# A four-layer graph kernel: the rank stage two blocks behind, its helpers on other engines, and the second table after the sums

## The chip, the cores and the metric

One core of one Trainium2 chip runs the whole kernel. The metric is the device time of one execution in microseconds (us); lower is better. Five engines work side by side, each through its own instructions in order: PE (TensorE matmuls; PEld are its weight loads), DVE (VectorE), ACT (ScalarE), POOL (GpSimd) and SP (SyncE, which only issues transfers here).

## What is computed

Four graph layers on 2708 nodes with 128 features and a dense 0/1 adjacency matrix A. Each layer normalises x over its features, takes the positive part, h, and adds a layer's result to x: first a graph attention, then a symmetric graph convolution, then a convolution with batch normalisation, and last a full attention. The diff touches the last one:

```
h  = max(layernorm(x), 0)
XW = h @ W
c  = XW @ a[:128];   r = XW @ a[128:]
Z1[i, j] = leaky_relu(r[i] + c[j], slope 0.01)
den = exp(Z1);   num = A @ den
att = where(num != 0, den / num, 0)
x   = x + A @ (att @ XW)
```

A @ den would be a product of 2708^3. The kernel sorts the nodes by r instead: for a given c[j] the nodes fall into those with r + c above zero and those below, and apart from the chunk of 124 nodes in which the border lies, whole chunks enter with one exponential each. So it needs the rank of each node in r, sums of A over chunks of the sorted nodes, and tables that say which rows of A to gather for each group of columns.

## The kernel before, in words

Nodes lie in T = 22 tiles of 128 (the last has 20) and NB = 6 blocks of four tiles (the last has two). Layers 0 to 2 (lines 256 to 911) stream A and its transpose in, keep the transpose as 8-bit numbers in SBUF (`adjt8`) and store it to DRAM; they end with layer 2's totals at 329 us. Nothing in them is touched. Then three stages of layer 3 follow.

**Rank stage** (lines 1123 to 1166, 329 to 398 us). The list is written by hand: everything in the `in_order()` block keeps, on each engine, the order in which the code issues it. For a block b:

- `relu_z(b)` (ACT, L963) applies layer 2's batch normalisation to a tile z of 512 columns, `turn_z(b)` (PE, L184) transposes it into PSUM bank 0, `refresh(b)` (DVE, L974 to L985) adds it to x and takes mean and variance; POOL takes the power -1/2 (L157).
- `centred(b)` (ACT, L991, four instructions) makes h, `turn_h3(b)` (PE, L180) transposes it, `project(b)` copies it out of PSUM (ACT, L1002, the tile hT) and multiplies by W and a (PE, L1008).
- `scores(b)` (DVE, L1015) leaves c and r. `factors(b)` (ACT L1046, POOL L1047) makes the scale of XW, `values3(b)` (ACT, L1054, four instructions, then a store on SP) writes XW to DRAM.
- `diag_of(b)` (POOL, L1027) puts r on a diagonal, `broadcast_r(b)` (PE, L1037, then ACT, L1040) spreads it into `row_b`, so that every partition has all r's so far. `lower_half(b)` (POOL, L1067) masks the block's own part, and `own_bits(b)` (DVE, L1079) compares it.
- `compared(t)` compares tile t's r with all earlier nodes (DVE, L1088, `bits`, three buffers). PE sums those bits over the columns' side (L1091, L1095); the sum over the rows' side is PE's for the tiles in FOLDED (L1104, L1112, read by `row_sums`, L1116) and ACT's for the others (L1107, `junk`): tiles 9, 11, 13, 15, 17, 19, 20 and 21.

In the loop (L1136 to L1165) round b projects block b and compares the tiles of block b - 1, whose `lower` was made in round b - 1; `refresh(b + 1)` stands on DVE behind `own_bits(b - 1)`. The first three blocks' z are made ahead.

**Table stage** (lines 1182 to 1486, 398 to about 466 us). This part isn't ordered by hand; a scheduler orders each engine's list. `pieces` splits a column of numbers of 32 bits into two or three of 16 (DVE, L1174 and L1178), so that products with 0/1 rows keep their precision. From the counts come `rank` (L1201 to L1209), `less` and `more` (chunk borders below or above the rank), and the weights `wts` (L1217, L1218: 22 tiles x 21 borders, six times). `sums` (PE, L1234: 132 matmuls of 450 or 452 columns) multiplies them with `adjt8`; they stand in four groups: tiles 0 to 7 early, tiles 8 to 15 after the first table, tiles 16 to 21 pair by pair of PSUM banks at the end. In between:

- the ranks' border values (`edge_v`, `edges`), how many columns fall to each chunk (`ohb`, `many`, PE L1246; `pre`, L1249 and L1251), and a chain of small DVE instructions that lays the columns out in 22 groups (L1269 to L1365), with four small matmuls (L1322, L1339) and one (L1359) in it;
- the first table: `lanes_of` makes for each tile a matrix of 128 x 128 zeros and ones (DVE, L1392, 22 instructions), `spread` the values beside it (`rhs_k`, L1398), PE multiplies them (L1410, L1414), and `row_i` (L1415) says which rows of A the POOL gathers fetch;
- the second table, the same for c (`lanes_j`, `rhs_j`, L1429, then `jt`, `c_tab`, `c_two`), stored as `ctwo_d` by SP (L1452) and read back in rows by `fetch_c` (SP, L1550);
- the chunk sums: per pair of banks a copy out of PSUM (`s_sb`, L1468, one on DVE, one on ACT), a matmul that joins the three pieces (L1469), two copies `flat` (ACT, L1475), a split in `pre_hi` and `pre_lo` (DVE, L1476, L1477), and four stores to `pre_d`, two on SP's queue and two on ACT's (L1481).

**Gather loop** (lines 1582 to 1660, 466 to 660 us). For each of the 22 groups POOL gathers rows of A (`g`, two per group, six buffers), chunk sums (`r`, from `pre_d`), and rows of XW (L1491); DVE widens g into r (L1569); ACT makes the exponentials of the first four rows from `diag` (DVE L1532, PE L1539, ACT L1510 and L1513, DVE L1522 to L1526), and PE multiplies (L1623, L1577). The last product with A follows (660 to 780 us).

Of the kernel before, what the change touches and what calls it, by code (L numbers as in the profile page):

```python
# [20 lines left out]
def binary(  # L21
# [68 lines left out]
    def acc_bank(b):  # L90
        return ps_acc.tile([P, 512], F32, tag=f"acc{b}", name=f"acc{b}")
# [854 lines left out]
    def row(name, n=NC, dtype=F32):  # L946
        return tab.tile([P, n], dtype, name=name)
# [9 lines left out]
    def relu_z(b):  # L957
        lo, hi = E0[b]
        n = len(TILES[b])
        zs3[b] = z = tabs.tile([P, 512], F32, tag="z", name="z")  # L960
        if hi - lo < n * P:
            nc.gpsimd.memset(z[:, hi - lo :], 0.0)
        nc.scalar.activation(z[:, : hi - lo], row_b[:, lo:hi], AF.Relu, bias=tot[:, 6:7], scale=tot[:, 5:6])  # L963
# [94 lines left out]

    rk = acc_bank(5)
# [63 lines left out]
    with in_order():  # L1123
        nc.vector.tensor_scalar_mul(tot[:, 2:3], tot[:, 0:1], -1.0)
        nc.vector.tensor_mul(tot[:, 5:6], vecs[:, 2:3], tot[:, 4:5])
        ts_(tot[:, 6:7], tot[:, 5:6], tot[:, 2:3], vecs[:, 3:4], ALU.mult, ALU.add)
        nc.tensor.matmul(rk[:NB, :], none_b, ones_b[:, None, :].to_broadcast([P, 4, P]), start=True, stop=False)
        nc.vector.memset(rowsum, 0.0)
        relu_z(0)
        turn_z(0)  # L1130
        relu_z(1)
        refresh(0)
        turn_z(1)
        centred(0)
        turn_h3(0)
        for b in range(NB + 1):  # L1136
            todo = list(TILES[b - 1]) if b else []
            if b < NB:
                project(b)
            if todo:  # L1140
                own_bits(b - 1)
                compared(todo.pop(0))
            if b + 2 < NB:
                relu_z(b + 2)
            if b + 1 < NB:
                refresh(b + 1)
                centred(b + 1)
            if b + 2 < NB:
                turn_z(b + 2)
            if b < NB:  # L1150
                scores(b)
                factors(b)
                diag_of(b)
                broadcast_r(b)
                lower_half(b)
            if todo:
                compared(todo.pop(0))
            if b + 1 < NB:
                turn_h3(b + 1)
            if b < NB:  # L1160
                values3(b)
            while todo:
                compared(todo.pop(0))
            if b > 1:
                row_sums(b - 2)  # L1165
        row_sums(NB - 1)
# [3 lines left out]
    def pieces(name, x, n):  # L1170
        out = []
        for i in range(n):
            h = tab.tile([P, T], BF16, name=f"{name}{i}")
            nc.vector.tensor_copy(h, x)  # L1174
            out.append(h)
            if i < n - 1:
                rest = tab.tile([P, T], F32, name=f"{name}r{i}")
                nc.vector.tensor_sub(rest, x, h)  # L1178
                x = rest
        return out  # L1180

    nc.scalar.activation(r_exp, r_of, AF.Exp)
    r_low = row("r_low", T)
    nc.scalar.activation(r_low, r_of, AF.Exp, scale=0.01)
    low_p = pieces("low_p", r_low, 3)
    exp_p = pieces("exp_p", r_exp, 3)
    node_v = tt("node_v", [P, T], node, valid, ALU.mult)
    node_p = pieces("node_p", node_v, 2)
    r_p = pieces("r_p", r_of, 3)
    c_p = pieces("c_p", c_col, 3)  # L1190
# [20 lines left out]
    less = tt("less", [P, T, NC + 1], over(rank, NC + 1), along(by_ch, NC + 1), ALU.is_lt, BF16)  # L1211
    more = tab.tile([P, T, NW], BF16, name="more")
    ts_(more, less[:, :, 1:NC], -1.0, 1.0, ALU.mult, ALU.add)
    wts = tab.tile([P, T, 6 * NW], BF16, name="wts")
    for i in range(3):
        o = 2 * NW * i
        nc.vector.tensor_mul(wts[:, :, o : o + NW], less[:, :, 1:NC], over(low_p[i], NW))  # L1217
        nc.vector.tensor_mul(wts[:, :, o + NW : o + 2 * NW], more, over(exp_p[i], NW))  # L1218
# [170 lines left out]
    def lanes_of(name, slot):  # L1389
        o = tab.tile([P, T, P], BF16, name=name)  # L1390
        for t in range(T):
            ts_(o[:, t, :], lane_b, slot[:, t : t + 1], None, ALU.is_equal)  # L1392
        return o
# [10 lines left out]
    slot_k = row("slot_k", T)  # L1404
    nc.vector.scalar_tensor_tensor(slot_k, nth, float(-CH), rank, ALU.mult, ALU.add)
    lanes_k = lanes_of("lanes_k", slot_k)
# [13 lines left out]

    ohst = tt("ohst", [P, T, NE], over(step, NE), along(lane[:, :NE], NE), ALU.is_equal, BF16)
    chunk1 = row("chunk1", T)
    nc.vector.tensor_reduce(chunk1, gej[:, :, :NC], AX.X, ALU.add)
    chunk_p = pieces("chunk_p", chunk1, 1)
    lanes_j = lanes_of("lanes_j", slot_j)
    rhs_j = spread("rhs_j", ohst, c_p + node_p + chunk_p)
    p = bank()
    for t in range(T):
        nc.tensor.matmul(p[:, : 6 * NC], lanes_j[:, t, :], rhs_j[:, t, :], start=(t == 0), stop=(t == T - 1))  # L1429
    jt = row("jt", 6 * NC)  # L1430
    nc.vector.tensor_copy(jt, p[:, : 6 * NC])
    c_tab = row("c_tab")
    nc.vector.tensor_reduce(c_tab, jt[:, : 3 * NC].rearrange("p (i b) -> p b i", b=NC), AX.X, ALU.add)
    c_chunk = jt[:, 5 * NC :]
    second = tt("second", [P, NE], chunk[:, :, 1], c_chunk, ALU.is_equal)
    gone = tt("gone", [P, NE], c_tab, second, ALU.mult)
    nc.vector.tensor_sub(c_two[:, :, 0], c_tab, gone)
    nc.vector.scalar_tensor_tensor(c_two[:, :, 0], second, -3.0e4, c_two[:, :, 0], ALU.mult, ALU.add)
    ts_(second, second, -1.0, 3.0e4, ALU.add, ALU.mult)
    nc.vector.tensor_add(c_two[:, :, 1], gone, second)  # L1440
    c_two_f = c_two.rearrange("p e h -> p (e h)")
    nc.scalar.activation(sig, c_tab, AF.Exp, scale=0.99)
    empty = row("empty")
    ts_(empty, c_chunk, 0.0, float(N), ALU.is_equal, ALU.mult)
    node_f = tt("node_f", [P, NE], jt[:, 3 * NC : 4 * NC], jt[:, 4 * NC : 5 * NC], ALU.add)
    nc.vector.tensor_add(xw_i, node_f, empty)
    FIRST = 4
    p = bank()
    nc.tensor.transpose(p[:NS, :P], c_two_f, ident)
    ctwo_t = row("ctwo_t", P)  # L1450
    nc.scalar.copy(ctwo_t[:NS], p[:NS, :P])
    nc.sync.dma_start(ctwo_d.rearrange("(s q) -> s q", q=P), ctwo_t[:NS])  # L1452
# [8 lines left out]
    for i, pair in enumerate(pairs):  # L1461
# [16 lines left out]
        for o, part_sb in ((0, pre_hi), (2 * NC, pre_lo)):  # L1478
            for h, queue in enumerate((nc.sync, nc.scalar)):
                x0 = h * HALF + lo  # L1480
                queue.dma_start(  # L1481
                    pre_d[o : o + 2 * NC, x0 : x0 + w].bitcast(F32), part_sb[64 * h : 64 * h + 2 * NC, lo:hi]
                )
    nc.scalar.activation(row_b[:, :N], row_b[:, :N], AF.Exp, scale=-0.99)
# [659 lines left out]
```

## Time and profile before

| | us |
|---|---|
| three runs: lowest, median, highest | 781.95, 782.66, 789.66 |
| the profiled execution | 782.27 |
| its span in the profile | 780.5 |
| rank stage, 329 to 398 | 69 |
| table stage, 398 to 466 | 68 |
| gather loop, 466 to 660 | 194 |

The page gives each engine's busy time, the span in forty slices, and the costliest groups of instructions. A group's line has the source line, the engine, the operation, the tile written and those read, and the count. Lines of the waits have the engine and instruction that waited, what released it, the total, the count and the longest. The chain of work that ended last is followed back from the end and is told in order of time: start, length, what. Most lines of the kernel lie in helpers (L937 is `tt`, L157 is `inv_sqrt`), so groups are read by tile as well.

### The profile page before, as it was taken

Reading aid. Unit: us, or ns where it says so; the run is one execution under the profiler, and the core shown is the slowest. Engines: PE = TensorE matmul, PEld = TensorE weight load, DVE = VectorE, ACT = ScalarE, POOL = GpSimd, SP = SyncE. Lnnn points to the kernel's source line nnn. Section 1 sums busy time; section 2 is a strip of 40 time slices with the busy share of each in tenths; the row PEclk is TensorE's granted clock in tenths of the full one; section 3 lists DMA queues with packets and bytes.
Section 4 is the critical chain, followed back from the end, with each engine's and each line's share of the span. In section 5 each row is a group of like instructions: output and inputs, shape, how many; then the busy total and the mean of one; then the engine's idle time right before and its main releaser. Section 6 shows DMA issues by size and latency. Waiting matters only on the chain.

```text
span 780.5 us, 8324 instructions
## 1 busy us (share of the span) xinstructions
PE 661.7 (85%) x2754; PEld 416.9 (53%) x2754; DVE 586.7 (75%) x1068; ACT 452.2 (58%) x658; POOL 263.2 (34%) x218
## 2 busy tenths in 40 slices
PE   5899969878899989657749948889899999999995
PEld 3433324326687767434426615556555556667784
DVE  5999779869857966536779757776877778876972
ACT  5667677558847644244560128758667667764442
POOL 3320000231102100034410547887777777600000
PEclk9999999999999999978978959989999999999997
DMA  9699999468244797000000425556665655759702
GB/s 339 246 396 424 424 426 383 184 249 305 118 179 158 258 353 249 1 14 28 27 8 1 106 82 140 157 147 153 159 165 119 146 152 158 186 161 336 276 26 63
DMA packets 49734, 146.29 MB, mean 187 GB/s; under 512 B 13602, under 2 KB 28446, under 8 KB 41254
## 3 DMA queue, kind: packets, MB, share of 16 engines
q1 hardware_dynamic: 28966, 85.11, 30.9%
q10 hardware_dynamic: 4684, 34.73, 12.5%
q0 software_dynamic: 16032, 25.83, 12.4%
q8 instruction: 24, 0.39, 0.2%
q14 instruction: 28, 0.23, 0.1%
HBM read 126.81 MB, written 18.77 MB: 187 GB/s over the span
## 4 chain that ended last, share of the span: by engine, by line
PE 25%; DVE 21%; issue 18%; DMA 16%; ACT 7%; POOL 6%; POOLq 0%; ACTq 0%; DVEq 0%
DMA g<-adjt_d,row_i 11%; PE acc L614 7%; PE acc L1739 6%; DVE chk L695 3%; DVE r L1569 3%; PE acc L1577 3%; PE bank L1623 3%; DVE m L483 2%; DMA adj_d<-a 2%; DVE e L1602 2%; DMA r<-pre_d,pre_i 2%; PE acc L1234 2%; ACT y L474 1%; POOL rstd L157 1%; ACT adjt L216 1%
## 5 line engine op out<-in xcount | busy, mean ns | idle before, releaser
L1623 PE MATMUL bank<-r,d_hi 128*128 128x512 f32 (+1 forms) x264 | 143.8, 549 | 25.1 <-DMA r<-pre_d,pre_i 14.5
L1624 ACT ACTIVATE ln<-bank,tiny 128x512 f32<-128x512 f32 x132 | 83.8, 634 | 71.9 <-PE bank L1623 33.1
L1577 PE MATMUL acc<-e,xw 128*128 128x512 f32 (+1 forms) x264 | 122.2, 551 | 0.0
L340 PE MATMUL acc<-tau,hw 128*128 128x512 f32 (+1 forms) x240 | 100.0, 563 | 12.4 <-DVE tau L348 12.3
L1491 POOL DMA_INDIRECT g<-adjt_d,row_i x44 | 86.6, 1968 | 39.1 <-DVE row_i L1415 26.0
L1623 PE MATMUL bank<-r,d_lo 128*128 128x512 f32 (+1 forms) x264 | 99.3, 380 | 0.0
L1569 DVE CAST r<-g 124x2708 fp32r<-124x2708 fp8e4 x44 | 68.0, 1573 | 41.4 <-DMA g<-adjt_d,row_i 11.3
L1623 PEld LDWEIGHTS bank<-r,d_hi 128*128 128x128 f32 x264 | 51.0, 193 | 67.4 <-issue 34.4
L481 ACT CAST m<-a 128x660 fp32r<-128x660 fp8e4 (+1 forms) x45 | 55.2, 1233 | 53.4 <-PE acc L1739 31.2
L340 PEld LDWEIGHTS acc<-tau,hw 128*128 128x128 f32 x240 | 43.6, 193 | 70.5 <-issue 44.2
L1491 POOL DMA_INDIRECT r<-pre_d,pre_i x44 | 64.8, 1474 | 47.5 <-PE bank L1623 22.4
L348 DVE SCALAR_TENSOR_TENSOR tau<-row_b,sg,a 128x1536 f32<-128x1536 f32 (+1 forms) x44 | 70.8, 1624 | 11.9 <-DMA a<-in_adj_dram 11.9
L1602 DVE SCALAR_TENSOR_TENSOR e<-row_b,sig,ln 128x1536 f32<-128x1536 f32 (+3 forms) x46 | 71.5, 1561 | 7.6 <-PE bank L1623 6.1
L157 POOL TENSOR_TENSOR rstd<-isq,neg_half 128x4 f32<-128x4 f32 (+1 forms) x24 | 29.1, 1214 | 128.3 <-DVE isq L156 83.6
L371 ACT ACTIVATE a<-a 128x2708 fp8e4<-128x2708 f32 x22 | 54.1, 2458 | 24.1 <-issue 11.3
L695 DVE SCALAR_TENSOR_TENSOR chk<-chk 128x2708 f32<-128x2708 f32 (+1 forms) x22 | 65.6, 2982 | 3.0 <-DMA chk<-in_adj_t_dram 3.0
L1623 PEld LDWEIGHTS bank<-r,d_lo 128*128 128x128 f32 x264 | 51.0, 193 | 28.7 <-issue 24.4
L1596 ACT ACTIVATE ln<-ln 128x512 f32<-128x512 f32 (+2 forms) x68 | 62.8, 926 | 0.6 <-ACT ln L1624 0.6
L1577 PEld LDWEIGHTS acc<-e,xw 128*128 128x128 f32 x264 | 48.4, 191 | 12.8 <-issue 3.8
L483 DVE CAST m<-a 128x2048 fp32r<-128x2048 fp8e4 (+1 forms) x43 | 39.5, 920 | 20.8 <-PE acc L614 10.8
L614 PE MATMUL acc<-m,y_hi 128*128 128x512 f32 (+1 forms) x132 | 49.8, 384 | 5.2 <-DVE m L600 2.0
L614 PE MATMUL acc<-m,h_hi 128*128 128x512 f32 (+1 forms) x132 | 53.8, 415 | 0.1
(438 smaller groups left out, 1259.9 us busy)
## 6 DMA issues: line engine op xcount, KB each, us to landing
a<-in_adj_dram SPq DMA_DIRECT2D x21, 1354.0 KB
adjt<-in_adj_t_dram ACTq DMA_DIRECT2D x12, 1354.0 KB
chk<-in_adj_t_dram ACTq DMA_DIRECT2D x11, 1354.0 KB
chk<-in_adj_t_dram SPq DMA_DIRECT2D x10, 1354.0 KB
a<-in_adj_t_dram SPq DMA_DIRECT2D x9, 1354.0 KB
adj_d<-a POOLq DMA_DIRECT2D x22, 338.5 KB
adjt_d<-adjt SPq DMA_DIRECT2D x5, 1354.0 KB
a<-adj_d SPq DMA_DIRECT2D x5, 1024.0 KB
```

Source lines behind the costliest of these rows:

```text
L340: nc.tensor.matmul(accs[b][:, : hi - lo], stationary, tau[b // 3][:, o : o + hi - lo], start=first, stop=last)
L348: nc.vector.scalar_tensor_tensor(tau, row_b[:, h0:h1], sg[:, t : t + 1], tiles_a[t][:, h0:h1], ALU.max, ALU.mult)
L481: nc.scalar.copy(m[:, : hi - lo], src[:, lo:hi])
L614: nc.tensor.matmul(sums_of[phase, b][:, : hi - lo], part[:, t, :], tiles_m[k][:, lo - base : hi - base], start=t == 0 and i == 0, stop=t = ...
L695: lambda: nc.vector.scalar_tensor_tensor(a[:r], a[:r], 1.0, a[:r], ALU.is_equal, ALU.not_equal, accum_out=odd[:r, t : t + 1])
L1491: return nc.gpsimd.indirect_dma_start(out=out, out_offset=None, in_=src, in_offset=bass.IndirectOffsetOnAxis(ap=idx, axis=0),)
L1569: ins = nc.vector.tensor_copy(rows_r[q][:CH], g[:CH])
L1577: m = nc.tensor.matmul(ys_acc[b][:, : hi - lo], xws[s], waiting[s][:, lo:hi], start=(s == 0), stop=(s == NE - 1))
L1596: pin(nc.scalar.activation(lns[s][:, lo:hi], lns[s][:, lo:hi], AF.Exp, scale=-1.0))
L1602: nc.vector.scalar_tensor_tensor(waiting[s][:, lo:hi], row_b[:, lo:hi], sig[:, s : s + 1], lns[s][:, lo:hi], ALU.max, ALU.mult)
L1623: pin(nc.tensor.matmul(num[:, : hi - lo], d, a[:, lo:hi], start=(i == 0), stop=(i == 3)))
L1624: pin(nc.scalar.activation(lns[s][:, lo:hi], num[:, : hi - lo], AF.Ln, bias=tiny))
```

## The change

Five edits, all between the end of layer 2 and the gather loop:

1. The rank stage's loop runs over i from -3 to NB + 1. Round i projects block i, centres block i + 1, refreshes block i + 2, makes z of block i + 3 and compares block i - 2. z has one buffer, not two. In a round the first comparison follows the projection, the second stands ahead of the broadcast, and `diag_of` stands ahead of `factors`.
2. `pieces` runs on POOL. Those of r and c are issued inside the last rounds, from i = NB on, those of the node numbers ahead of the stage.
3. `less`, `more` and `wts` are made for tiles 0 to 7 and then for tiles 8 to 21.
4. `lanes_of` makes the rows of the first n_act tiles on ACT: |lane - slot| for each tile, then max(1 - that, 0) in one instruction. All 22 of the first table, 14 of the second.
5. The block that builds the second table stands behind the pairs of sums and their stores, not ahead of them.

Its core (the moved block of the second table is left out where it is unchanged):

```diff
-        zs3[b] = z = tabs.tile([P, 512], F32, tag="z", name="z")
+        zs3[b] = z = tabs.tile([P, 512], F32, tag="z", name="z", bufs=1)
...
+    def pieces(name, x, n):
...
+            nc.gpsimd.tensor_copy(h, x)
...
+                nc.gpsimd.tensor_sub(rest, x, h)
...
+    r_low = row("r_low", T)
+    node_v = tt("node_v", [P, T], node, valid, ALU.mult)
+    node_p = pieces("node_p", node_v, 2)
...
-        relu_z(0)
-        turn_z(0)
-        relu_z(1)
-        refresh(0)
-        turn_z(1)
-        centred(0)
-        turn_h3(0)
-        for b in range(NB + 1):
-            todo = list(TILES[b - 1]) if b else []
-            if b < NB:
-                project(b)
+        for i in range(-3, NB + 2):
+            todo = list(TILES[i - 2]) if i > 1 else []
+            if 0 <= i < NB:
+                project(i)
+            if -1 <= i < NB - 1:
+                centred(i + 1)
             if todo:
-                own_bits(b - 1)
+                own_bits(i - 2)
                 compared(todo.pop(0))
-            if b + 2 < NB:
-                relu_z(b + 2)
-            if b + 1 < NB:
-                refresh(b + 1)
-                centred(b + 1)
-            if b + 2 < NB:
-                turn_z(b + 2)
-            if b < NB:
-                scores(b)
-                factors(b)
-                diag_of(b)
-                broadcast_r(b)
-                lower_half(b)
+            if i + 3 < NB:
+                relu_z(i + 3)
+            if 0 <= i < NB:
+                scores(i)
+                diag_of(i)
+                factors(i)
+            if 0 <= i + 2 < NB:
+                refresh(i + 2)
+            if i + 3 < NB:
+                turn_z(i + 3)
             if todo:
                 compared(todo.pop(0))
-            if b + 1 < NB:
-                turn_h3(b + 1)
-            if b < NB:
-                values3(b)
+            if 0 <= i < NB:
+                broadcast_r(i)
+                lower_half(i)
+            if -1 <= i < NB - 1:
+                turn_h3(i + 1)
+            if 0 <= i < NB:
+                values3(i)
+            if i == NB:
+                nc.scalar.activation(r_exp, r_of, AF.Exp)
+                nc.scalar.activation(r_low, r_of, AF.Exp, scale=0.01)
+                low_p = pieces("low_p", r_low, 3)
+                exp_p = pieces("exp_p", r_exp, 3)
+                r_p = pieces("r_p", r_of, 3)
+                c_p = pieces("c_p", c_col, 3)
             while todo:
                 compared(todo.pop(0))
-            if b > 1:
-                row_sums(b - 2)
+            if i > 2:
+                row_sums(i - 3)
...
+    for ts in (slice(0, 8), slice(8, T)):
+        n = ts.stop - ts.start
...
+        nc.vector.tensor_tensor(
+            less[:, ts], each(rank, NC + 1), by_ch[:, None, :].to_broadcast([P, n, NC + 1]), ALU.is_lt
+        )
+        ts_(more[:, ts], less[:, ts, 1:NC], -1.0, 1.0, ALU.mult, ALU.add)
+        for i in range(3):
+            o = 2 * NW * i
+            nc.vector.tensor_mul(wts[:, ts, o : o + NW], less[:, ts, 1:NC], each(low_p[i], NW))
+            nc.vector.tensor_mul(wts[:, ts, o + NW : o + 2 * NW], more[:, ts], each(exp_p[i], NW))
...
-    def lanes_of(name, slot):
+    def lanes_of(name, minus_slot, n_act, slot=None):
...
-        for t in range(T):
+        far_off = tab.tile([P, T, P], BF16, tag="far_off", name="far_off")
+        for t in range(n_act):
+            nc.scalar.activation(far_off[:, t, :], lane, AF.Abs, bias=minus_slot[:, t : t + 1])
+        nc.scalar.activation(o[:, :n_act, :], far_off[:, :n_act, :], AF.Relu, bias=ones[:, 0:1], scale=-1.0)
+        for t in range(n_act, T):
             ts_(o[:, t, :], lane_b, slot[:, t : t + 1], None, ALU.is_equal)
...
-    lanes_k = lanes_of("lanes_k", slot_k)
+    lanes_k = lanes_of("lanes_k", minus_k, T)
...
+    lanes_j = lanes_of("lanes_j", minus_j, 14, slot_j)
```

On the engines' lists this leaves, in the end: on ACT the last count (`junk` of tile 21) still stands behind the exponential of row_b (L1484), as before; on PE 30 sums stand ahead of the matmuls of `many` (11 before) and 18 between those of `pre` and L1322 (37 before); 54 follow the first table without a break, then pair 0's join, 14 sums, pair 1's, 7 sums, pair 2's, and only then the second table's products. On DVE the copy `s_sb` of pair 0 stands behind the last `rhs_j`, and `jt` between `pre_hi` and `pre_lo` of pair 2. On SP the six stores to `pre_d` stand ahead of that of `ctwo_d`.

## The prediction, made before the changed kernel ran

> **What bounds the kernel now.** I read the page for the whole, then the windows for the stages, then the waits and the chain inside the two stages that the diff touches. Times are microseconds from the start of the span; a letter in brackets is a block (0 to 5) or a tile (0 to 21).
>
> ```profile
> span 780.5 us, 8324 instructions
> PE 661.7 (85%) x2754; PEld 416.9 (53%) x2754; DVE 586.7 (75%) x1068; ACT 452.2 (58%) x658; POOL 263.2 (34%) x218
> ...
> PEclk9999999999999999978978959989999999999997
> ```
>
> ```profile
> 329.00:398.00 69.00, 50.20 (x316) 28.07 (x316) 40.38 (x123) 36.63 (x85) 25.64 (x25) 0.85 0.07 22
> 398.00:420.00 22.00, 11.34 (x77) 7.47 (x77) 17.92 (x95) 5.36 (x5) 1.23 (x1) 0.69 0.00 1
> 420.00:440.00 20.00, 20.00 (x123) 14.29 (x122) 19.15 (x78) 0.80 (x2) 8.42 (x6) 1.00 0.23 54
> 440.00:460.00 20.00, 11.90 (x58) 4.95 (x56) 8.44 (x25) 6.42 (x15) 3.76 (x3) 0.79 0.37 109
> ```
>
> The windows' columns are length, then busy PE, PEld, DVE, ACT, POOL, then clock and DMA. Rank stage (329 to 398) and table stage (398 to 466) take 137 us in which no engine is full except PE and DVE at 420 to 440. They are bound by handing over:
>
> ```profile
> DVE own L1079 <- POOL lower L1067: 19.2, 6, 5.2
> ACT row_b L1040 <- PE acc L1037: 19.2, 6, 3.9
> ...
> PE acc L1037 <- POOL diag L1027: 12.6, 6, 3.4
> ```
>
> Vector waits 19.2 of 69 us for the GpSimd half-matrix of the block just projected; what stands behind that wait is `refresh` of the next block, so all engines turn in one ring per block (the six `own` start at 343.12, 352.00, 361.17, 371.66, 382.00, 391.74: 9.7 each). The chain shows what ends each stage:
>
> ```profile
> 398.02 2.35 ACT row_b L1484
> 400.37 2.44 ACT junk L1107 x2
> 403.66 0.69 DVE less L937
> ...
> 417.30 7.17 PE acc L1234 x37
> ...
> 438.06 3.43 DVE rhs_j L1398 x6
> ...
> 455.31 2.25 DMA pre_d<-pre_lo
> ...
> 459.76 6.28 DMA r<-pre_d,pre_i
> ```
>
> The rank waits for the last count on ScalarE (to 402.8); I call the start of `less` R (403.66). Then R+20.7 (424.40) is the matmul pair L1322 behind 37 sums; R+25.9 is `row_i` (429.51); R+37.7 the end of `rhs_j` (441.40); R+51.6 the end of the last `pre_lo` (455.28); R+61.1 (464.78) the first matmul of the gather loop, R+62.5 that of its second row.
>
> **Part 1, comparisons two blocks behind.** Vector no longer meets a half-matrix made in the same round: `own` finds one that is a round old. The 19.2 us go, and the next ring limits. I follow it by the start of the copy hT (L1002), with durations of the DVE, ACT and PE rows. z has now one buffer: z(1) waits for the transposes of z(0) (331.3), z(2) stands on ACT behind four `centred` (334.65), and its transposes (to 336.6) stand on PE ahead of those of h(0): hT(0) goes from 335.30 to 337.65, a loss of 2.35. Round 0 then is hT 0.6, projection 2.1 (half clock, as in the row at 335.94), scores 0.3, the add of refresh(2) 0.7, transposes of z(3) 0.6, broadcast 1.1, copy row_b 0.55, four xw 1.1 = 7.05: hT(1) 344.7. Round 1 has the projection at 1.1 and the rest alike: 6.0, hT(2) 350.7. In round 2 the second comparison stands ahead of the broadcast and its bits behind refresh(4): 6.0 - 0.65 + 1.4 + 0.3 + 0.3 = 7.35, hT(3) 358.05. Round 3: refresh(5) 1.35, bits 0.55, comparison 0.95 in place of the add and transposes: 7.55, hT(4) 365.6. Round 4: tile 7 is still on PE (projection ends 367.5), tiles 8 and 9 2.0, broadcast behind a slowed diagonal 1.25, row_b 0.6, xw 1.15, the count of tile 11 1.4 ahead of the copy: hT(5) 373.9. Before it was 384.81. Round 5 is PE: 0.45 + 0.7 + tiles 12, 13 2.65 + broadcast 0.7 + tiles 14, 15 3.1, to 381.5; Vector has bits of 16 at 381.8, of 19 at 386.2, of 20 at 388.8, of 21 at 390.4. On ScalarE: count of 19 from 386.25 to 388.5, count of 20 388.85 to 391.2, the exponential of row_b 2.4, the last count 2.45: 396.1 in place of 402.8. The order of those last two doesn't change. So -6.6.
>
> The row against a rule: after an idle of 2.12 us on PE the row at 370.43 gives four transposes 1.06, the one at 344.62 (the same work at full clock) 0.61. The Trainium skill (TensorE: Matmul & The Clock Gate, Part 1) wants an idle window of some 3.4 us for the half clock. My rounds leave PE idle for 1.7 to 2.1 at most. By the rule nothing is lost after round 0, by the row each such gap can cost about 1.6 (3.2 us at half rate). I charge 1.0: rank stage -5.6 (by the rule -6.6, by the row at three gaps -1.8).
>
> **Part 2, the 16-bit pieces on GpSimd.** Twenty Vector instructions leave the end of the stage, about 0.085 apart, 1.7 us. Worth nothing: Vector there waited 2.74 us for the last count. They come back as twenty GpSimd instructions of 22 columns from 385.6 on (when r_exp is there), ten of them ahead of the weights at R. The Trainium skill (GPSIMD Engine Reference, the opening ahead of section 1) calls GpSimd the wrong place for elementwise work, about half of Vector's rate; that is 20 x 0.33 = 6.6 from Vector's 0.16. The trace has `factor` (4 columns) at 0.20 alone and 1.37 beside Vector's bits: 4 to 27 us in all, the first ten 2 to 14. I take 1.4 until the bits end (390.4) and 0.35 after: the ten end at 393, R is 397. Cost nothing while the ten end before R; if the cover were gone, R moves by the excess.
>
> **Part 3, weights for eight tiles first.** less 0.24 + 0.37, more 0.17, six products of 168 columns at 0.23: the first sum starts at R+2.4 and not R+4.8. The second halves cost six more starts, and `edge_v` ends at R+7.6, not R+6.7; `many` goes from R+11.2 to R+11.8. But PE now has 30 of the 48 first sums done ahead of `many` (11 before), the first ten at half clock (0.4), the others 0.2; so L1322 has 18 ahead of it, not 37: R+14.2 + 18 x 0.2 = R+17.8, and Vector's part is ready at R+16. Gain 2.9.
>
> **Part 4, unit rows on ScalarE.** lanes_k leaves Vector (22 x 0.165 = 3.6). On ScalarE 22 Abs of 128 columns at 0.3 (as L991, four in 1.28), pre_sb between, one Relu of 2816 columns 2.55: from R+8.3 to R+18.1; its matmuls come at R+20.6. Hidden by 2.5; without that cover each us would go to row_i. `row_i` R+22.9. For lanes_j eight stay on Vector (1.3), 14 Abs and a Relu of 1792 (4.2 + 1.7) end at R+32.7, beside Vector's rhs_j to R+32.2 (5.5 earlier).
>
> **Part 5, all sums, then the second table.** PE has 54 sums in a row (10.5 from R+22.7), so pair 0 is done at R+32.7, and the copies s_sb wait for Vector's rhs_j and ScalarE's Relu, both to about the same instant. Then pair 0: joint 0.9, flat 1.1, pre_hi 0.4, pre_lo 0.6 to R+36.0; pair 1's joint after 14 sums at R+37.85; the last sums at R+39.2, s_sb R+39.9, joint R+40.85, flat R+41.9, pre_hi, jt, pre_lo: R+43.25 for R+51.6. Before, the copy s_sb of pair 2 stood on ScalarE behind a DMA issue that waited for pre_lo (2.15); now only that of pre_hi(1) is ahead. The six pre_d stores on SP and six on ScalarE's queue go out ahead of ctwo_d on SP: ctwo_d is late by 3 against R, but its readers c_row (SP) wait for it only till R+47.7, needed at about R+58. What is late next is the second table: jt R+42.4, c_two R+44.7, diag there, and from diag to the second d_lo 7.05 as before (455.38 to 462.4): R+51.75, widen(0) R+53.3. The gather of r starts behind the matmul L1539 as its row says (R+47.9) and lands 6.0 later: R+53.9. First loop matmul R+54.0 for R+61.1: -7.1, say -7.0 with the instant where three engines meet.
>
> **Sum.** -5.6 - 7.0 = -12.6. From 466 on nothing changes, and the first gathers of g are issued 9 us earlier, with more lead. Against the profiled execution (782.27, of which the span is 780.5) that makes 769.7; its time is 0.4 below the median shown (782.66), so 770.1 on the median. 1% is 7.8 us, about what can be told from no change.
>
> **Rivals.** (a) 48%: the sum, 770.1 (767 to 774). (b) 18%: more. No clock loss (-6.6), the r gather waits for its stores alone (R+46.5, 1.4 sooner, with widen(0) at R+53.3 then the limit): -14.5, 768; up to 763 if lanes and sums meet better. (c) 22%: part of it is lost. Either PE falls to half clock in three rounds (-1.8 for the rank), or the gather loop gives some back: the chain from 470 to 560 is 32.7% gathers of g, single ones 5.9 to 14.6 us, so an earlier start needn't come through whole. -5 to -9: 774 to 778. Against it: the gathers are issued when the loop frees their buffers, so they move with it. (d) 6%: no change, if the stage was bound by the counts on ScalarE (14.9 us of `junk` plus 2.4) all along; against it, ScalarE is 36.6 of 69 busy. 782. (e) 6%: slower, by GpSimd: `pow` on 22 columns took 3.88 there. At 3.5 each the first ten end at 420.6, R would be 23 later than planned: 793. It decides from 2.5 each (ten from 385.6 to 410.6, which eats the 12.6); the nearest rows say 0.2 to 1.4.
>
> Range 764 to 778: (a), (b) and most of (c). Faster by over 1% (below 774.8): (a), (b) and a third of (c), 0.75; within 1%: 0.18; slower: 0.07.
>
> **What would show it.** Waits of own for lower near nothing; hT(5) at about 374; last `junk` ending at 396 to 397; a first sum 2.4 after less; L1322's successor 17.8, row_i 22.9, last pre_lo 43 and the first loop matmul 54 after less. Wrong if PE's clock in the rank stage falls below 0.85, if `wts` waits for GpSimd, if s_sb waits for ScalarE's Abs, or if the loop is longer than its 194 us (466 to 660).

## The result, and the profile after

| | before | after |
|---|---|---|
| median of 13 runs each (lowest to highest), us | 783.54 (777.24 to 789.66) | 773.99 (768.75 to 781.47) |
| ratio after to before | | 0.9882, 95% interval 0.9848 to 0.9915 |
| the profiled execution, us | 782.27 | 772.65 |
| its span | 780.5 | 770.9 |

The change saves 1.2%, about 9.3 us. The prediction had 12.6 us (770.1). A few executions of each kernel take over 1.5% longer than its fastest, and the ratios leave them out; the one profiled with edit 3 undone (784.2 us) is of these.

Line numbers from here on are those of the kernel whose trace is shown, mostly the changed one; behind line 1059 most lie 5 to 17 above the ones used so far, and those of the pairs of sums 23 below.

The head of the changed kernel's page, engine by engine, and the row of the granted clock:

```profile
span 770.9 us, 8331 instructions
...
PE 664.5 (86%) x2754; PEld 419.4 (54%) x2754; DVE 580.9 (75%) x1017; ACT 467.6 (61%) x696; POOL 276.7 (36%) x242
...
PEclk9999998989999999957979969999999999899998
```

Work has moved from VectorE (586.7 to 580.9 us busy) to ScalarE (452.2 to 467.6) and GpSimd (263.2 to 276.7). The four windows of the prediction, now of the changed kernel (length, then busy PE, PEld, DVE, ACT, POOL, then clock, DMA share, GB/s):

```profile
329.00:398.00 69.00, 51.88 (x320) 30.05 (x320) 41.07 (x115) 40.90 (x86) 32.24 (x46) 0.80 0.07 22
398.00:420.00 22.00, 18.04 (x114) 12.36 (x115) 19.76 (x99) 10.16 (x26) 1.48 (x2) 0.80 0.00 1
420.00:440.00 20.00, 19.31 (x110) 12.01 (x109) 14.20 (x43) 9.71 (x23) 11.39 (x6) 1.00 0.37 102
440.00:460.00 20.00, 8.37 (x38) 4.92 (x39) 11.72 (x25) 5.58 (x15) 10.26 (x7) 0.69 0.34 84
```

From 398 to 420 PE is busy 18.0 us and not 11.3: the sums start sooner. But in the rank stage the granted clock is 0.80, where it was 0.85. The waits of that stage (who waited for what: total, times, longest) no longer have a line of `own` for `lower`, which was the longest before. What has grown is VectorE's wait for PE's projection. The line before, then three lines of the changed kernel:

```profile
DVE rc L1015 <- PE bank L1008: 5.7, 6, 2.1
```

```profile
DVE rc L1015 <- PE bank L1008: 21.5, 11, 4.5
ACT row_b L1040 <- PE acc L1037: 15.1, 5, 4.5
POOL diag L1027 <- DVE rc L1015: 10.3, 5, 3.9
```

ScalarE's wait for the broadcast (`row_b`) isn't new, it was 19.2.

At the far end, PE's list in order of time shows how the gather loop starts (start, length, line, what; in brackets the idle time ahead of it and what ended it):

```profile
446.09 1.12 PE L1551 MATMUL bank<-diag,ones 128*128 128x512 f32 x2 [0.77 <-DVE diag L1544]
453.90 0.76 PE L1635 MATMUL bank<-r,d_hi 128*128 128x512 f32 x1 [6.69 <-DMA r<-pre_d,pre_i]
...
456.88 0.77 PE L1635 MATMUL bank<-r,d_hi 128*128 128x512 f32 x1 [1.79 <-DMA r<-pre_d,pre_i]
```

The first matmul of the loop's second row, 456.88, stood at 466.18 before:

```profile
466.18 0.77 PE L1623 MATMUL bank<-r,d_hi 128*128 128x512 f32 x1 [0.21 <-DMA r<-pre_d,pre_i]
```

It comes 9.3 us sooner. From there to the end of the span it is 314.0 us, and it was 314.3. So in this pair of traces what was won ahead of the loop came through.

Two marks make runs comparable, as single executions differ by up to 4 us before the rank stage and by several us behind the loop's start: the time from the first z (the start of `relu_z(0)` on ScalarE) to R (the start of `less` on VectorE), and that from R to the matmul of the second row.

| us | before | predicted | after |
|---|---|---|---|
| first z to R | 74.34 | 68.7 | 69.35 |
| R to first sum | 4.8 | 2.4 | 2.7 |
| R to the row behind L1327 | 21.6 | 17.8 or just after | 18.6 |
| R to row_i | 25.9 | 22.9 | 22.8 |
| R to the end of rhs_j | 37.8 | 32.2 | 31.9 |
| R to the end of the last pre_lo | 51.6 | 43.25 | 44.3 |
| R to the first r gather | 54.9 | 47.9 | 48.05 |
| R to the second row | 62.5 | 55.4 | 57.6 |

### The profile page after: what moved, and what is told of

It reads as the page before. It is cut to its first block, busy times and chain, and to the rows that moved or that the text cites. A ratio compares the mean times of both kernels' runs of the same rounds, so it can differ in the third digit from the quotient of the medians.

```text
span 770.9 us, 8331 instructions
## 1 busy us (share of the span) xinstructions
PE 664.5 (86%) x2754; PEld 419.4 (54%) x2754; DVE 580.9 (75%) x1017; ACT 467.6 (61%) x696; POOL 276.7 (36%) x242
## 5 line engine op out<-in xcount | busy, mean ns | idle before, releaser
L340 PE MATMUL acc<-tau,hw 128*128 128x512 f32 (+1 forms) x240 | 101.8, 572 | 12.7 <-DVE tau L348 12.7
L1503 POOL DMA_INDIRECT g<-adjt_d,row_i x44 | 91.8, 2086 | 23.4 <-issue 12.5
L1635 PEld LDWEIGHTS bank<-r,d_hi 128*128 128x128 f32 x264 | 51.5, 195 | 66.3 <-issue 32.2
L1503 POOL DMA_INDIRECT r<-pre_d,pre_i x44 | 59.3, 1348 | 36.9 <-PE bank L1635 14.7
L483 DVE CAST m<-a 128x2048 fp32r<-128x2048 fp8e4 (+1 forms) x43 | 39.5, 920 | 18.9 <-PE acc L614 8.8
L372 POOL DMA_DIRECT2D adj_d<-a x22 | 12.3, 558 | 115.0 <-ACT a L371 115.0
```

The costliest lines, as they stand in the source:

```text
L340: nc.tensor.matmul(accs[b][:, : hi - lo], stationary, tau[b // 3][:, o : o + hi - lo], start=first, stop=last)
L1503: return nc.gpsimd.indirect_dma_start(out=out, out_offset=None, in_=src, in_offset=bass.IndirectOffsetOnAxis(ap=idx, axis=0),)
L1635: pin(nc.tensor.matmul(num[:, : hi - lo], d, a[:, lo:hi], start=(i == 0), stop=(i == 3)))
```

## The experiments

The theory to test: the sum was right in its parts, and what is missing was lost in two places, PE's half clock in the first rounds and the landing of the second r gather. The rivals are in the expectations. Each kernel was also timed against the kernel before (783.2 to 784.0 in these groups).

### PE kept busy in the first rounds

```diff
+    def warm(n):
+        for _ in range(n):
+            nc.tensor.matmul(
+                rk[:NB, :], none_b, ones_b[:, None, :].to_broadcast([P, 4, P]), start=False, stop=False
+            )
...
+        warm(14)
         nc.vector.memset(rowsum, 0.0)
...
                 project(i)
+                if i < 3:
+                    warm(4)
...
                 turn_z(i + 3)
+                if i < -1:
+                    warm(4 * (i + 4))
...
                 turn_h3(i + 1)
+                if i < 3:
+                    warm(5)
```

> The changed kernel with TensorE kept busy through the first rounds of the rank stage by matmuls of zero weights into the bank of counts (adding nothing): 14 ahead of the first z, 4 to 12 behind each of the first transposes, 4 behind each projection and 5 behind the transposes of h, in rounds 0 to 2. Theory 1 (the rank stage fell short of the sum because TensorE ran at half clock in rounds 0 to 2, granted clock 0.50 to 0.84 from 329 to 360): the projection of round 0 takes 1.1 and not 2.1, the transposes 0.6 and not 1.08, the broadcasts 1.1 and not 1.91; the last hT comes 3 to 5 us earlier than 376.7, R (the start of less, 399.28) comes 2 to 4 us earlier, and the time is 770 to 772 where the changed kernel has 774. Theory 2 (ScalarE's order sets the rounds: copy of row_b, four xw, then hT, whatever the clock): the last hT and R move by less than 1 us and the time is 774 within 1.

Measured: 770.41, ratio 0.9799 (0.9734 to 0.9865). First z to R 64.05, 5.3 less than in the changed kernel's trace. PE's list of the changed kernel:

```profile
330.80 1.11 PE L184 MATMUL acc<-ident,z 128*128 128x128 f32 x4 [3.69 <-ACT z L963]
...
338.74 2.10 PE L1008 MATMUL bank<-w_ext,hT 128*128 128x130 f32 x8 [0.68 <-ACT hT L1002]
341.78 1.08 PE L184 MATMUL acc<-ident,z 128*128 128x128 f32 x4 [0.94 <-DVE xs L974]
342.65 1.91 PE L1037 MATMUL acc<-diag,ones 128*128 128x512 f32 x2
...
346.76 1.16 PE L1008 MATMUL bank<-w_ext,hT 128*128 128x130 f32 x8 [1.34 <-ACT hT L1002]
348.86 1.08 PE L184 MATMUL acc<-ident,z 128*128 128x128 f32 x4 [0.94 <-DVE xs L974]
```

And the same work with the zero weights in between (L1140 are the added matmuls):

```profile
338.39 1.16 PE L1008 MATMUL bank<-w_ext,hT 128*128 128x130 f32 x8
339.48 1.03 PE L1140 MATMUL acc<-ones_b,none_b 128*6 128x512 bf16 x4
340.49 0.63 PE L184 MATMUL acc<-ident,z 128*128 128x128 f32 x4
340.98 1.12 PE L1037 MATMUL acc<-diag,ones 128*128 128x512 f32 x2
```

Each instruction takes about half: 2.10 to 1.16, 1.08 to 0.63, 1.91 to 1.12. The windows from 330 to 345 and from 345 to 362 have a clock (the third number from the end) of 0.50 and 0.70 in the changed kernel, and of 1.00 here; the first two lines are the changed kernel's:

```profile
330.00:345.00 15.00, 9.52 (x33) 6.91 (x34) 6.40 (x35) 6.61 (x15) 4.24 (x5) 0.50 0.01 1
345.00:362.00 17.00, 11.93 (x49) 6.58 (x48) 7.00 (x32) 9.48 (x31) 8.96 (x10) 0.70 0.10 31
```

```profile
330.00:345.00 15.00, 12.99 (x70) 6.48 (x68) 6.76 (x38) 9.12 (x24) 5.47 (x6) 1.00 0.02 7
345.00:362.00 17.00, 14.36 (x92) 7.65 (x90) 10.29 (x46) 8.44 (x27) 9.79 (x12) 1.00 0.14 42
```

Theory 1 holds: added work makes the stage shorter, because the rounds wait for PE. VectorE's wait for the projection falls from 21.5 to 16.7 us.

The start of the hT copies, from the first z, shows the rounds:

| us from the first z | hT(0) | (1) | (2) | (3) | (4) | (5) | R |
|---|---|---|---|---|---|---|---|
| before | 6.0 | 13.3 | 22.1 | 31.7 | 44.3 | 55.5 | 74.3 |
| predicted, without the charge for the clock | 8.3 | 15.4 | 21.4 | 28.7 | 36.3 | 44.6 | 67.7 |
| after | 8.2 | 16.2 | 23.3 | 31.5 | 38.9 | 46.8 | 69.35 |
| after, PE kept busy | 6.8 | 13.2 | 19.0 | 26.2 | 33.6 | 41.4 | 64.05 |

At full clock the rounds last 6.3, 5.9, 7.2, 7.4 and 7.8 us; the sum had 7.05 (its projection at half clock), 6.0, 7.35, 7.55 and 8.3.

### The same matmuls in the old loop

The edit is the same `warm`, at the same places of the old loop of the kernel before.

> The kernel before with the same matmuls of zero weights in the first three rounds of its old loop, nothing else. From the first z to R it had 74.34. Theory 1 (edit 1's own worth is what the sum said, 5.6 to 6.6, at full clock, and the half clock takes 2.5 of it away in the changed kernel, but less in the old loop, whose ring of VectorE and GpSimd has slack for TensorE): 71.5 to 74 from the first z to R, against 64.05 of the changed loop with the same matmuls, so edit 1 is worth 7.5 to 10 at full clock; 781 to 783.5. Rival (the clock is worth the same 6 us in either loop): 67.5 to 69, and 777 to 778.

Measured: first z to R 74.13, where it was 74.34, though the clock from 330 to 345 is 1.00 now and was 0.70. VectorE still waits for GpSimd's half-matrix, 20.0 us for 19.2:

```profile
DVE own L1079 <- POOL lower L1067: 20.0, 6, 5.0
```

Theory 1 holds for the stage: the old ring of VectorE and GpSimd covered PE's half clock, the new one has no such cover. At full clock edit 1 is worth 74.13 - 64.05 = 10.1 us, more than the sum had.

The time is another matter: 777.75, ratio 0.9955 (0.9931 to 0.9979), is the rival's 777 to 778, some 3.5 us less than before, and in the trace only 0.6 of that lies ahead of the second row. What made the rest isn't settled. Behind the second row the four traces with zero weights have 308 to 311.5 us, the others 309.8 to 319.3 (318.5, that with edit 3 undone, among them). So of what the zero weights save in the time, here and in the changed kernel, only the part in the marks is accounted for.

### Edit 1 alone, and all but edit 1

The first is the kernel before with the new loop and `bufs=1` for z. The second is the changed kernel with the old loop, in whose last round the pieces are issued:

```diff
-        for i in range(-3, NB + 2):
...
+        relu_z(0)
+        turn_z(0)
+        relu_z(1)
+        refresh(0)
+        turn_z(1)
+        centred(0)
+        turn_h3(0)
+        for b in range(NB + 1):
...
+            if b == NB:
+                nc.scalar.activation(r_exp, r_of, AF.Exp)
...
+                c_p = pieces("c_p", c_col, 3)
             while todo:
```

> The kernel before with edit 1 alone (the new loop and the single z). The 16-bit pieces stay on VectorE behind the stage, the tables as before. Theory 1 (the five edits add up, edit 1 is worth what the trace of the changed kernel shows at R): R 398.7 to 399.9 for 403.66, the second row of the gather loop at 461.2 to 462.4 (466.18 before), 778.5 to 779.5 where the kernel before has 783.5. Rival (the pieces of VectorE, 1.7 us, come onto the path as VectorE is full from 380 to 395 in the new order): R at 400.5 to 401.5 and 780 to 781.

> The changed kernel with the rank stage's loop as before (comparisons one block behind; z has one buffer, as two don't fit beside edit 2's tiles), edits 2 to 5 kept. Theory 1: R at 403.5 to 404.5, from R to the second row of the gather loop 57 to 58 us as in the changed kernel (57.6; 62.5 before), 778 to 779.5. Rival (the pieces on GpSimd need the new order: in the old one they stand behind the last lower of the ring and end after the last count): the weights wait for GpSimd and R to the first sum takes over 3 us; 780 or more.

Measured: edit 1 alone 778.17, ratio 0.9936 (0.9908 to 0.9964), first z to R 71.53; all but edit 1 782.1, ratio 0.9969 (0.9937 to 1.0001), first z to R 74.77 and R to the second row 60.2.

Edit 1 alone gives 5.0 us in the time. R follows the last count by 0.87 us, as before (0.86), so VectorE's 16-bit pieces did not come onto the path, and the rival is out. In its trace the stage gained only 2.8, at a clock of 0.59 and 0.50 in the two windows. Six traces of the new loop without zero weights and with the exponential in its place have 67.83 to 71.53 from the first z to R, mean 69.9; three of the old loop (one with zero weights) have 74.13 to 74.77, mean 74.4. So edit 1 is worth 4.5 on average, and it varies by 3.7 from execution to execution; the old loop varies by 0.6. The stage follows the clock from 345 to 362: 67.83 us at 0.87, 69.01 and 69.35 at 0.70, 70.74 and 70.83 at 0.60, 71.53 at 0.50.

Without edit 1, the other four gave 2.4 us (the interval runs from 4.9 to nothing), where 4 to 5.5 were expected, and R to the second row is 60.2 and not 57 to 58. The rival of this run has its mechanism shown, at a smaller price than the 3 us that it named: GpSimd's list and VectorE's behind R (405.19).

```profile
404.49 1.23 POOL L1442 MEMSET flat<- 128x1354 f32 x1 [11.16 <-ACT junk L1122]
405.66 0.34 POOL L1063 CAST low_p<-r_low 128x22 bf16<-128x22 f32 x1
```

```profile
406.75 0.34 DVE L1227 TENSOR_TENSOR wts<-less,low_p 128x168 bf16<-128x168 bf16 x1 [0.38 <-POOL low_p L1063]
407.62 0.33 DVE L1228 TENSOR_TENSOR wts<-more,exp_p 128x168 bf16<-128x168 bf16 x1 [0.52 <-POOL exp_p L1063]
408.34 0.34 DVE L1228 TENSOR_TENSOR wts<-more,exp_p 128x168 bf16<-128x168 bf16 x1 [0.39 <-POOL exp_p L1063]
```

In this order of GpSimd's list the memset of `flat` stands ahead of the pieces, and it waits for the last count. The pieces start 0.5 behind R, the weights wait for them, and the first sum comes at R + 4.3 and not R + 2.7. This is the cover that the prediction named for edit 2 (the ten pieces end before R): in the changed kernel the tenth ends at 393.96, 5.3 ahead of R, though one of them took 1.59 us:

```profile
391.23 1.59 POOL L1063 CAST exp_p<-r_exp 128x22 bf16<-128x22 f32 x1
...
393.76 0.20 POOL L1063 CAST exp_p<-exp_pr 128x22 bf16<-128x22 f32 x1
```

### The exponential behind the last count

```diff
         row_sums(NB - 1)
+        nc.scalar.activation(row_b[:, :N], row_b[:, :N], AF.Exp, scale=-0.99)
...
-    nc.scalar.activation(row_b[:, :N], row_b[:, :N], AF.Exp, scale=-0.99)
```

> The changed kernel with the exponential of row_b (2.44 us of ScalarE, which stands ahead of the last count) behind the last count. Theory 1 (the end of the rank stage is ScalarE's chain of counts): the last count ends at 396.1 and not 398.5, R comes 2.4 us earlier, and the whole of it reaches the end: 771.6 where the changed kernel has 774. Rival (VectorE's bits or the 16-bit pieces on GpSimd end about there too): R gains less than 1 us and the time stays at 774 within 1. Rival 2 (the tables take up the gain, since ScalarE starts the unit rows later): R gains 2.4 but the first matmul of the second row of the gather loop less than 1.2.

Measured: 774.17, ratio 0.9877 (0.9826 to 0.9927), no difference from the changed kernel that these intervals can show. The end of ScalarE's list in the changed kernel, and then in this one:

```profile
393.65 2.44 ACT L1496 ACTIVATE row_b<-row_b 128x2708 f32<-128x2708 f32 x1
396.00 2.43 ACT L1122 ACTIVATE junk<-bits 20x2688 bf16<-20x2688 bf16 x1
```

```profile
396.34 2.44 ACT L1122 ACTIVATE junk<-bits 20x2688 bf16<-20x2688 bf16 x1
...
398.79 2.44 ACT L1184 ACTIVATE row_b<-row_b 128x2708 f32<-128x2708 f32 x1
```

From the copy hT(5) to R it is 20.4 where the changed kernel has 22.6: the 2.2 are there. But in this execution the rounds lasted 1.2 longer (half clock again), and the second row came at R + 58.4. From the first z to the second row only 0.25 us is left (126.70 for 126.95), less than the 1.2 of rival 2; but `row_i` stands at R + 22.8 as in the changed kernel, so its reason, later unit rows, isn't what took the gain. The place is shown, the worth in the time only together with the clock, below.

### Edits 2 to 5 undone one by one

Pieces on `nc.vector` behind the loop; `for ts in (slice(0, T),)` for the weights; `lanes_of` with `n_act` 0 and `slot_k`, `slot_j` again; the block of the second table moved ahead of `pairs`.

> The changed kernel with edit 2 undone: the 16-bit pieces on VectorE, issued behind the rank stage as before. Theory 1 (worth nothing in itself, VectorE waits for the last count on ScalarE): R comes where it did against the last count (0.76 behind it), from R to the first sum 2.7, to the second row of the gather loop 57.6, and 774 within 1.5. Rival (the twenty of VectorE, 1.7 us, come onto the path, as VectorE's bits now end later against the counts): R is 1 to 1.7 us later against the last count, 775 to 776.

> The changed kernel with edit 3 undone: less, more and the weights for all 22 tiles in one go. Theory 1: the first sum starts at R + 4.8 and not R + 2.7, many falls to R + 11.3, the row behind the matmuls L1327 comes at R + 21.5 and not R + 18.6, row_i at R + 25.7, and the second row of the gather loop at R + 60.5 and not R + 57.6; 777. Rival (with the unit rows on ScalarE, VectorE reaches many sooner and fewer first sums stand ahead of it): own_beg within 1 us of R + 18.6 and the time stays at 774 to 775.

> The changed kernel with edit 4 undone: all 44 unit rows on VectorE. Theory 1: the end of rhs_j goes from R + 31.9 to R + 34.2 to R + 37.5 (14 instructions at 0.165 for certain, the other 22 as far as VectorE had no wait there), and the second row of the loop moves as much, 2.3 to 5.6 us: 776 to 779. Rival (lanes_k lies in VectorE's wait for the matmuls L1327, and ScalarE's two Relu of 2.6 and 1.7 us set as much as they save): less than 1.5 us, 774 to 775.

> The changed kernel with edit 5 undone: the second table ahead of the pairs of sums. Theory 1 (edit 5 brings the last pre_lo forward by what the table cost the pairs, but puts the second table last): the last pre_lo comes at R + 45 to R + 46 for R + 44.3, the r gathers go out at R + 48.5 to R + 49.5 for R + 48.05, but c_two is done by R + 36, so that the row behind them is as in the kernel before, 10.9 behind the last pre_lo, at R + 56 to R + 57: edit 5 is worth nothing or costs 1 us, 773 to 774. Rival (the sum as predicted, edit 5 carries the gain of the last pre_lo): the last pre_lo at R + 48 to R + 51, the second row of the loop at R + 60 to R + 62, 777 to 779.

| undone | time, ratio (interval) | R to row behind L1327 | end of rhs_j | last pre_lo | first r gather | second row | first r gather to second row |
|---|---|---|---|---|---|---|---|
| none | 773.99, 0.9882 (0.9848 to 0.9915) | 18.6 | 31.9 | 44.3 | 48.05 | 57.6 | 9.55 |
| 2, pieces | 774.71, 0.9878 (0.9847 to 0.9909) | 18.6 | 32.2 | 44.4 | 47.8 | 58.0 | 10.1 |
| 3, weights | 776.46, 0.9900 (0.9824 to 0.9975) | 21.9 | 35.2 | 47.6 | 51.4 | 60.9 | 9.5 |
| 4, unit rows | 776.52, 0.9900 (0.9859 to 0.9941) | 18.9 | 38.7 | 44.4 | 47.6 | 58.0 | 10.5 |
| 5, table last | 775.21, 0.9894 (0.9864 to 0.9923) | 18.8 | 32.2 | 46.6 | 50.5 | 58.4 | 7.9 |

The times differ by less than their intervals; the marks decide. With edit 3 undone only the marks from R are used. They agree with the two other kernels that make the weights in one go, the kernel before and that with edit 1 alone: the first sum at R + 4.8 in all three, the row behind L1327 (L1322, L1317) at R + 21.9, 21.6 and 21.6.

Edit 2 is worth nothing, as the sum had it: R is 0.77 behind the last count and was 0.76, and the 0.4 at the second row lies in the landing of the gathers (last column). Edit 3 is worth 3.3 us (60.9 - 57.6), for 2.9 in the sum: with it undone, PE does 35 sums without a break ahead of the matmuls L1327.

```profile
417.14 6.93 PE L1239 MATMUL acc<-adjt,wts 128*126 128x452 fp8e4 x35
424.00 0.40 PE L1327 MATMUL bank<-ahead,ones 22*128 22x22 f32 x2
```

Edit 4 is worth 0.4 at the second row once edit 5 is there, and that too lies in the landing: undone, the gathers go out 0.45 sooner. So its rival holds in the marks (less than 1.5). Undone, rhs_j ends 6.8 later, but that costs nothing ahead of the last pre_lo, as VectorE's list then has the copies of the sums in between the rhs_j:

```profile
434.69 0.65 DVE L1404 TENSOR_TENSOR rhs_j<-ohst,c_p 128x484 bf16<-128x484 bf16 x1
435.26 0.62 DVE L1441 COPY s_sb<-acc 126x452 f32<-126x452 f32 x1
435.80 1.22 DVE L1404 TENSOR_TENSOR rhs_j<-ohst,c_p 128x484 bf16<-128x484 bf16 x2
```

Edit 5 brings the last pre_lo and the r gathers forward by 2.4 us, and the second row by 0.8 only; R + 58.4 lies between what theory 1 (56 to 57) and the rival (60 to 62) had. Between the two stands the landing of the gathers: 7.9 us from issue to use with the table early (7.3 to 7.6 in three traces with the old order of the tables), 9.3 to 10.5 in eight traces with the table last.

### The c_row reads behind the gathers

With the table last, SyncE issues the first read of `c_row` and GpSimd the first gather of r within 0.4 us of each other. SyncE's list, then GpSimd's, in the changed kernel:

```profile
446.99 0.35 SPq L1562 DMA_DIRECT2D c_row<-ctwo_d  x1
```

```profile
447.33 0.89 POOL L1503 DMA_INDIRECT r<-pre_d,pre_i  x1 [11.78 <-PE bank L1551]
448.53 0.88 POOL L1503 DMA_INDIRECT r<-pre_d,pre_i  x1 [0.30 <-issue]
```

The reads lead by 0.34 us here, and with edit 4 undone by -0.17. Where the landing took 7.3 to 7.9, they led by 1.0 (before, edit 1 alone) or 3.5 (table early). The edit:

```diff
-        nc.sync.dma_start(p, ctwo_d[s0 * P : (s0 + 2) * P].partition_broadcast(P))
+        src = ctwo_d[s0 * P : (s0 + 2) * P].partition_broadcast(P)
+        if pool:
+            pin(nc.gpsimd.dma_start(p, src))
+        else:
+            nc.sync.dma_start(p, src)
...
-        fetch_c(FIRST + 2 * s)
+        fetch_c(FIRST + 2 * s, True)
...
-            fetch_c(coming + 4)
+            fetch_c(coming + 4, s == 0)
```

> The changed kernel with the first three reads of c_row (128 KB each) issued by GpSimd behind the four gathers of r and two of xw, not by SyncE at the same instant as the first r (446.99 and 447.33). Theory 1 (with edit 5 the second r gather lands 2 us later against its issue because the c_row reads lie ahead of it in the DMA queues): from the first issue of an r gather to the matmul of the second row 7 to 8 us, not 9.3 to 10.5, that row at R + 55.3 to R + 56 and 772 to 773. Rival (it is the gathers themselves, or the three c_row issues hold up GpSimd's next gathers): 9.3 to 10.5 as before, or the loop behind longer by 1 us or more; 774 to 775.5.

Measured: 773.11, ratio 0.9831 (0.9773 to 0.9889); the second row at R + 55.7, 7.6 behind the first gather. PE's list:

```profile
452.12 0.77 PE L1639 MATMUL bank<-r,d_hi 128*128 128x512 f32 x1 [5.77 <-DVE r L1585]
...
453.55 0.80 PE L1639 MATMUL bank<-r,d_hi 128*128 128x512 f32 x1 [0.24 <-DVE r L1585]
```

PE now waits for VectorE's widening of g (`r`, L1585) and no longer for the gather. Theory 1 holds for the mark. In the time the 1.9 us can't be told from the changed kernel; the stretch behind the second row was 319 us in this execution and 308 in the last kernel below, which has the same edit. One price shows: ScalarE now waits for c_row, 2.6 us here and 2.0 there, and starts the exponentials from it at R + 62.0 and R + 61.8, where the changed kernel had R + 61.1. Whether that takes part of the gain back isn't shown.

### The two together

The first has `warm` and the exponential last, the second the c_row reads too.

> The changed kernel with TensorE kept busy in the first rounds and the exponential of row_b behind the last count, both edits as run singly. If they add up (each acts at its own place: hT at the beginning, the last count at the end): from the first z to R 61.6 to 62.3 (64.05 with the first alone), 767.5 to 769.5. If VectorE's bits end the stage once the rounds are short: 63 to 64 and 770.

> As warm_exp, and the c_row reads behind the r gathers too. If the c_row reads delay the second r gather: 1.5 to 2 us less than warm_exp, 766 to 768. If not, the same as warm_exp within 1 us.

Measured: 762.17, ratio 0.9743 (0.9690 to 0.9795), and 763.04, ratio 0.9755 (0.9708 to 0.9803). First z to R is 61.87 and 61.84: the two edits of the rank stage add up (64.05 less 2.2). The second row comes 8.0 behind the first gather with the c_row reads behind, 10.1 without, and again the time doesn't show it. Both are faster than the changed kernel, whose interval begins at 0.9848, by about 1.3%. That is 3 to 5 us less time than was expected of them (767.5 to 769.5, 766 to 768); the marks don't account for it, as with the zero weights in the old loop.

## Why the prediction was right, and where it fell short

The sign and the range held: faster, 774.0 in 764 to 778. The time lies at the border of the sum's band (a) and of rival (c), a part lost, and of the signs of being wrong one came: the clock of the rank stage, 0.80 where 0.85 was the limit. Of the marks, hT(5) came at 376.7 for 374 and the last count at 398.5 for 396 to 397. (By its own chances faster by over 1% is 0.73, not 0.75.) Point by point:

- Part 1. The wait of `own` for `lower` is gone, and the last count sets R: right. The step that failed is "I charge 1.0". The prediction had the row (four transposes at 1.06 for 0.61 behind an idle of 2.12) and the rule of the Trainium skill (TensorE: Matmul & The Clock Gate, Part 1: half rate after an idle window of about 3.4 us, full again after as long a busy one), and took little from either. What it left out is the way back: it let each gap cost a fixed 1.6. PE was idle 3.69 us ahead of the first transposes, then every round kept it idle for 0.6 to 1.5 us, and it ran at half clock until 346. It was full for one projection after 3.6 us of unbroken work (341.78 to 345.4), half again two idles of 1.34 and 0.94 later, full for the next projection after 3.5 us (348.86 to 352.4), and half again. The busy part of the rule agrees with this, the idle part doesn't: no idle after the first was over 2.1. Nor did the half clock come with the idle itself: the first work behind it was still at full clock (the broadcasts at 368.44 before, the projection at 346.76 after), the slow transposes 2 us later. The right charge was 69.9 - 67.7 = 2.2 on average against the sum's own rounds, and 5.8 against rounds at full clock throughout (69.9 - 64.05), mostly because the sum also had half clock ahead of hT(0) and in round 0's projection. So the clock part of rival (c), given as -1.8 for the rank, came true in part: -4.5 on average for -5.6.
- Part 2. Worth nothing, cover as named; the run without edit 1 shows the price without it, 1.6 us. The 22-column operations took 0.20 to 0.31 alone and 1.37 and 1.59 beside VectorE's bits (389.68 to 392.74), close to the estimate of 0.35 and 1.4; the 0.33 from half of Vector's rate fits only those that ran alone.
- Part 3. The largest part of the tables: 3.3 for 2.9.
- Part 4. The sum gave it lanes_k and the earlier end of rhs_j. The end of rhs_j did move by 5.9, but with the table last nothing of the loop's start hangs on it; worth 0.4 at most.
- Part 5. The last pre_lo came at R + 44.3 (43.25), the gathers at R + 48.05 (47.9). The step that failed is "lands 6.0 later": the first landed 6.6 after its issue, and the second row was ready 9.55 after it, not 7.5, as the c_row reads came to lie beside them. The prediction had both instants, c_row's reads at R + 47.7 and the gathers at R + 47.9, and that the reads have time until R + 58; it put their meeting at nothing.
- "From 466 on nothing changes" held for the pair of traces, 314.0 us for 314.3. That it came out so close is in part luck, as this stretch lasts from 308 to 319 us in the other traces.

The two missed terms explain most of the difference, which is 3.0 between the pair of traces (12.6 less 9.6): 0.65 in the rank stage and 2.2 at the second row, with 0.6 lost upstream of both and 0.3 won behind. The averages over the traces put 1.1 in the rank stage and about 2.4 at the gathers.

## What to carry to other kernels

When a change takes away a wait that every engine shared, ask which engine was running slowly under its cover: here PE's half clock cost nothing in the old loop and 6 us in the new one, and zero-weight matmuls in its idle gaps took that back. A transfer that is moved "because it isn't needed yet" still goes out at some instant; look at what else is issued there. And undo edits one by one in the end: of five, two were worth 4.5 and 3.3 us in their marks, one 0.8, and two nothing that the scatter of the landing lets one see.

## What was not expected of the hardware

- PE was at half clock for most of three rounds with idle gaps of only 0.6 to 1.5 us between its work (0.50 from 330 to 345, 0.70 to 362), while 58 filling matmuls, some 13 us, kept it at 1.00 from 330 to 385. A filling matmul of 512 columns in 16 bits cost 0.23 us.
- Three reads of 128 KB, issued within 0.4 us of a small indirect gather, went with a use of its second piece that was about 2.4 us later; issuing them behind the gathers took that away, and where they led by 1.0 us or more it wasn't there. Which of the queues' steps does it isn't shown.
